# A perceiver block on one core: finer yields for VectorE and ScalarE in the first part, no clearing of the results' table, new estimates in the planner

## The chip, the cores and the metric

The kernel runs on 1 core of a Trainium2 chip. The metric is device time in microseconds (us) of one execution. TensorE is called PE (its weight loads PEld), VectorE DVE, ScalarE ACT, GpSimd POOL, SyncE SP; each has a queue of its own which it works off in order.

## The reference

All is float32. There are 16 sequences of 64 tokens with 256 features, 1024 tokens in all. Six residual steps follow one another:

```python
x = x + xattn0(layernorm(x), ctx)   # 1 head, masked, softmax over 1601 context rows
x = x + mla(layernorm(x))           # 16 heads of 16, causal over 64 tokens, rms-normed q and k
x = x + tile_ffn(layernorm(x))      # one of 8 tiles of weights by position
x = x + xattn1(layernorm(x), ctx)   # 1 head, softmax over 1601 context rows
x = x + ssm(layernorm(x))           # conv of 4, 8 heads, 64 states, selective scan
x = x + moe(layernorm(x))           # 64 experts, 8 of each token, and a shared one
```

The layer norm has no weights: `(x - mean) / sqrt(var + 1e-5)`. The ssm's step size is `dt = softplus(dt_proj + dt_bias)`. The experts compute `silu(x Wg) * (x Wu) Wd`, weighted by the router's normed scores.

## The kernel before, in words

The tokens are worked in 8 groups of 128 (two sequences each). In the first part, to about 600 us, a generator `chain(g)` carries a group through the first four steps: `query(g, "a")` (layer norm, the query transposed into the keys' space), `turn_ctx` for its two sequences' contexts, `cross(g, "a")` (scores, softmax, weighing of the context), `mla(g)`, `clear`, `ffn(g)`, `query(g, "b")`, `cross(g, "b")`. Names of buffers end in `_a` or `_b` for the two cross attentions, in `ml` for mla, `ff` for the tile ffn, `ss` for the ssm, `mo` for the experts. Within cross: `sc` scores, `pa` their exponentials (ACT), `pspa` and `paT` their transposes and the copies of them out of PSUM, `po` the weighed context, `oT` and `py` the output's transpose and product. In mla: `mqk` the normed q and k, `ms` scores, `mee` exponentials, `mpe` and `meT` their transposes, `mo` the result.

Two chains are alive at a time. Beside them run `prepare` (weights of the other steps) and, from group 6's end, `prepare_ssm`, which loads and turns the ssm's input weights (`wl` by SP, `ps_win` on PE), then `inlet(g)` (layer norm, input product, conv pieces `xc`, silu, transposes `ps_xt`) and `sums` (softplus of the step sizes as a polynomial, then `ps_seg` and `ps_sums`), which works on half of the groups at a time. After that come, for each group, the scan (`ps_g`, `gt`, `ps_y`), the routing of its tokens (`route`) and the shared expert; last the experts: the tokens' rows are scattered into a table `xbuf` in device memory (POOL), read back by expert (`xg`), multiplied, and the results scattered into a table `ybuf`, from which each token collects its eight rows.

Which instruction follows which on an engine is settled when the program is built, by a small planner, `drive` (L231). Each generator hands over at its `yield cost, gap`: `cost` is the estimate of the PE time of the piece just emitted, `gap` the estimate of the time until its next piece has its operands. The planner keeps a clock `now`, adds the cost to it, puts the generator aside for `gap`, and goes on with the first that is due:

```python
            c = next((c for c in free if c["at"] <= now), None) or min(free, key=lambda c: c["at"])
            now = max(now, c["at"])
            ...
            cost, gap, sign = (*got, "")[0:3]
            now += cost
            c["at"] = now + gap
```

A third value, "want" or "free", takes or gives back a right that one generator holds at a time. So a yield is at once an estimate and a place where other generators' instructions may come between; between two yields a generator's instructions stand together on every engine.

Lines that the change touches: `zero` and `clear` (L178 to L187: each chain clears, by SP, an eighth of `xbuf` in halves of rows, 544 bytes, and an eighth of `ybuf`, in rows' halves of 512 bytes, from a zero tile); `evac` (L191 to L197, copies out of PSUM turn about on DVE and ACT); `layernorm` (L199: bn_stats, bn_aggr and an add on DVE, a power on POOL for `rs`, then one DVE pass at L213 that waits for it); `inlet` (L267), `sums` (L309; the polynomial L333 to L335, `dt` L338, `ps_seg` L343); `query` (L533), `cross` (L562), its `turn` (L607), `weigh` (L617); `mla` (L742), `ffn` (L931), `chain` (L957), `prepare_ssm` (L986, the loads L997 and L1000, `ps_win` L1041), `route` (L1129).

Of the kernel before, what the change touches and what calls it, by code (L numbers as in the profile page):

```python
# [147 lines left out]
def perceiver_kernel(ctx: ExitStack, tc: tile.TileContext, a: dict, consts: bass.AP, out: bass.AP):  # L148
# [28 lines left out]

    zero = cst.tile([P, DX // 2], F32, name="zero")  # L178
    G.memset(zero, 0.0)
    xbuf0 = xbuf.rearrange("(p n) (c d) -> p (n c) d", p=P, c=2)  # L180
    ybuf0 = ybuf.rearrange("(p n) (c d) -> p (n c) d", p=P, c=2)

    def clear(lo, hi, stage):

        after(nc.sync.dma_start(out=xbuf0[:, 2 * lo : 2 * hi, :], in_=_bc(zero, 1, 2 * (hi - lo))), [stage])
        lo, hi = (n * NTOK * TOPK // NSLOT for n in (lo, hi))
        after(nc.sync.dma_start(out=ybuf0[:, 2 * lo : 2 * hi, :], in_=_bc(zero[:, 0 : D // 2], 1, 2 * (hi - lo))), [stage])  # L187

# [9 lines left out]

    def layernorm(src, name, xn, parted=False):  # L199
        st = small.tile([P, 6], F32, tag="ln_st", name=f"st_{name}")  # L200
        V.bn_stats(st, src)
        mv = small.tile([P, 2], F32, tag="ln_mv", name=f"mv_{name}")
        V.bn_aggr(mv, st)
        ve = small.tile([P, 1], F32, tag="ln_ve", name=f"ve_{name}")
        V.tensor_scalar(ve, mv[:, 1:2], 1e-5, None, ALU.add)  # L205
        rs = small.tile([P, 1], F32, tag="ln_rs", name=f"rs_{name}")
        G.tensor_tensor(rs, ve, neghalf[:, 0:1], ALU.pow)  # L207
# [5 lines left out]
        V.tensor_scalar(to, src, mv[:, 0:1], rs, ALU.subtract, ALU.mult)  # L213
        return xn

# [51 lines left out]
    def inlet(g, tile1, tile2):  # L267
        yield from until(lambda: "winT" in sw)
        xnT, winT = sw["xnT"], sw["winT"]
        tk = slice(g * P, (g + 1) * P)  # L270
        xn = layernorm(x[:, g, :], f"ss{g}", tile1([P, D], f"xn_ss{g}"))
        yield 0, 2.8
        pt = pst([P, 2, P], f"psx_ss{g}")
# [35 lines left out]
    def sums(lo, hi):  # L309

        yield from until(lambda: sw["done"] >= hi)
        dv = sw["dtr"][:, lo:hi, :].rearrange("p g n -> p (g n)")
        n = (hi - lo) * NH


        def sp(name):
            return sw["pool"].tile([P, n], F32, tag=f"sp_{name}", name=f"sp_{name}_{lo}")

        na = sp("na")
        V.scalar_tensor_tensor(na, dv, -1.0, dv, ALU.mult, ALU.min)  # L320
        u = sp("u")
        A.activation(u, na, AF.Exp)
        up2 = sp("up2")
        V.tensor_scalar(up2, u, 2.0, None, ALU.add)
# [12 lines left out]
        dt = sp("dt")  # L337
        V.scalar_tensor_tensor(dt, dv, 0.0, po, ALU.max, ALU.add)  # L338
        yield 0, 4.0
        sg = sw["pool"].tile([n, (NL + 1) * P], F32, tag="sg", name=f"sg_{lo}")  # L340
        for i, w in ((0, 512), (512, 384)):
            pm = psm([n, w], f"ps_seg_{lo}_{i}")
            T.matmul(pm, lhsT=dt, rhs=sw["kmat"][:, i : i + w], start=True, stop=True)  # L343
# [7 lines left out]
    with ExitStack() as p1:  # L351
# [181 lines left out]
        def query(g, lay, beside=None):  # L533
# [3 lines left out]
            xs = x[:, g, :]  # L537
            xn = layernorm(xs, f"xa{nm}", tile1([P, D], f"xn_{nm}"))
            if beside:
                yield from beside  # L540
            else:
                yield 0, 2.7
            xnT = turned(xn, f"xa{nm}")
# [15 lines left out]
            queries[g, lay] = qT, cc, xb  # L559
            yield 1.3, 0.2  # L560

        def cross(g, lay):  # L562
# [31 lines left out]
            for j in range(4):  # L594
# [12 lines left out]
            def turn(j):  # L607
# [47 lines left out]
            V.tensor_tensor(xs, py, xb, ALU.add)  # L655
            yield 0.45, 0

# [84 lines left out]
        def mla(g):  # L742
            wqk, wvo, wkr, vbs = wts["m"]
            xs = x[:, g, :]
            xn = layernorm(xs, f"ml{g}", tile1([P, D], f"xn_ml{g}"))
            yield 0, 2.7
            xnT = turned(xn, f"ml{g}")
# [3 lines left out]
            for c in range(2):  # L751
# [3 lines left out]
                pqs.append(pq)  # L755
            ms = small.tile([P, 32], F32, tag="mms", name=f"mms_{g}")
            V.reduce_sum(ms, sq.rearrange("p c (n d) -> p (c n) d", d=HD), AX.X)
            me = small.tile([P, 32], F32, tag="mme", name=f"mme_{g}")
            V.tensor_scalar(me, ms, 1.0 / HD, EPS_RMS, ALU.mult, ALU.add)

            rr = small.tile([P, 32], F32, tag="mrr", name=f"mrr_{g}")
            V.tensor_scalar(rr.bitcast(I32), me.bitcast(I32), -0.5, 1597463007.0, ALU.mult, ALU.add)
            for i in range(3):
                t = small.tile([P, 32], F32, tag="mt", name=f"mt_{g}_{i}")
                V.tensor_tensor(t, rr, rr, ALU.mult)
                V.scalar_tensor_tensor(t, t, -0.5, me, ALU.mult, ALU.mult)
                V.scalar_tensor_tensor(rr, t, 1.5, rr, ALU.add, ALU.mult)
            qk = tile2([P, 2, 2, P], f"mqk_{g}")
            for c in range(2):
                pv = pqs[c].rearrange("p (j n d) -> p j n d", j=3, d=HD)  # L770
                rv = rr.rearrange("p (c j n) -> p c j n", c=2, j=2)
                for j in range(2):
                    V.tensor_tensor(
                        qk[:, c, j, :].rearrange("p (n d) -> p n d", d=HD), pv[:, 2 * j, :, :], _bc(rv[:, c, j, :], 2, HD), ALU.mult
                    )
            yield 0.7, 0.1
            vs = []
            for c in range(2):
# [12 lines left out]
                vs.append(vb)  # L791
            yield 0.9, 5.0
            ptq = pst([P, 2, P], f"mtq_{g}")
# [22 lines left out]
            for c in range(2):  # L816
                for r in range(4):
                    for b in range(2):
# [5 lines left out]
                            stop=True,  # L824
                        )
            ees, eTs = [], []
            for i in range(2):
# [13 lines left out]
                ees.append(ee)  # L841
            yield 1.2, 3.8, "free"
            for i in range(2):
# [28 lines left out]
            V.tensor_tensor(xs, xs, y, ALU.add)  # L872
            yield 2.0, 0.8

# [56 lines left out]
        def ffn(g):  # L931
            fw, ohb, fb = wts["f"]
            xs = x[:, g, :]
            xn = layernorm(xs, f"ff{g}", tile1([P, D], f"xn_ff{g}"))
            yield 0, 2.7
            xnT = turned(xn, f"ff{g}")
# [192 lines left out]
    def route(g):  # L1129
# [506 lines left out]
```

## Time and profile before

| | us |
|---|---|
| runs | 1113.68, 1122.16, 1114.81; median 1114.81 |
| profiled execution | 1104.11, its span 1102.2 |
| PE busy (82% of the span) | 901.2 |
| PEld busy (62%) | 684.8 |
| DVE busy (54%) | 590.5 |
| POOL busy (25%) | 274.4 |
| ACT busy (25%) | 271.2 |
| mean granted PE clock | 0.879 of full |

An engine's busy time is the sum over its instructions; a wait is the idle time of an engine ahead of an instruction, named by the operation that released it. The profile's slices divide the span by 40, so that one slice is 27.6 us. The share of DMA is the mean busy share of the 16 DMA engines. The transfers that matter here, by their issues on SP: `xbuf<-zero`, 8 of 1632 KB, and `ybuf<-zero`, 8 of 1024 KB.

### The profile page before, as it was taken

What the parts mean: (1) busy time and instruction counts of PE and PEld (TensorE: products, weight loads), DVE (VectorE), ACT (ScalarE), POOL (GpSimd) and SP (SyncE); (2) the same over time, 40 slices, a digit from 0 to 9 for tenths busy, and PEclk for the clock granted to TensorE, in tenths of its full rate; (3) what the DMA queues carried; (4) which work ended last, traced back from release to release, by engine and by line L of the source; (5) the groups of instructions that cost most, each with busy time, mean ns of one, the idle gap of its engine ahead of it and who ended that gap; (6) DMA issues with size and microseconds to landing.
All of it is one profiled execution on the core that took longest, in us unless ns stands there. A gap on an engine that the chain in (4) does not pass through costs nothing. (4 is left out here: it accounts for less than half of the span.)

```text
span 1102.2 us, 16572 instructions
## 1 busy us (share of the span) xinstructions
PE 901.2 (82%) x6242; PEld 684.8 (62%) x6242; DVE 590.5 (54%) x1823; ACT 271.2 (25%) x592; POOL 274.4 (25%) x326
## 2 busy tenths in 40 slices
PE   4887889978799788979867569999999449999955
PEld 3665656645656456556554458888888338888834
DVE  1346454356545554364535874976867773343316
ACT  0213132321332222331313543222210013233310
POOL 0000101001000001001010222266665524655650
PEclk7878998989999899999978878887867669999988
DMA  6411324303613307103430073544411877989336
GB/s 235 172 38 62 100 89 130 120 2 99 184 36 120 97 4 219 59 2 100 103 91 11 28 153 84 118 113 113 113 42 41 277 263 241 304 282 296 116 119 269
DMA packets 99511, 138.99 MB, mean 126 GB/s; under 512 B 10211, under 2 KB 85407, under 8 KB 96358
## 3 DMA queue, kind: packets, MB, share of 16 engines
q1 hardware_dynamic: 84816, 116.36, 34.8%
q0 software_dynamic: 7680, 17.33, 4.6%
q10 hardware_dynamic: 6934, 4.23, 1.5%
q8 instruction: 50, 0.82, 0.3%
q14 instruction: 31, 0.25, 0.1%
HBM read 97.54 MB, written 44.53 MB: 129 GB/s over the span
## 5 line engine op out<-in xcount | busy, mean ns | idle before, releaser
L1481 POOL DMA_INDIRECT ybuf<-yo,goal x96 | 93.5, 974 | 81.3 <-ACT yo L1507 32.7
L1473 PE MATMUL ps_ee<-xT,wq 128*128 128x192 f32 x512 | 96.1, 331 | 0.0
L1115 POOL DMA_INDIRECT xbuf<-xtok,idx x64 | 70.0, 1094 | 71.3 <-DVE idx L1205 48.1
L1473 PEld LDWEIGHTS ps_ee<-xT,wq 128*128 128x128 f32 x512 | 82.5, 191 | 6.5 <-issue 5.0
L620 PE MATMUL po_a<-cn,paT_a 128*64 128x256 f32 (+1 forms) x416 | 59.5, 424 | 22.6 <-ACT mee L840 19.2
L207 POOL TENSOR_TENSOR rs_ff<-ve_ff,neghalf 128x1 f32<-128x1 f32 x8 | 4.4, 548 | 219.1 <-DVE ve_ff L205 211.6
L946 PE MATMUL fpy<-fw,fxm 128*128 128x256 f32 x256 | 58.3, 387 | 0.7 <-DVE fxm L943 0.7
L1337 PEld LDWEIGHTS ps_g<-pc,pb 64*128 64x128 f32 x768 | 51.8, 207 | 10.4 <-issue 5.1
L620 PE MATMUL po_b<-cn,paT_b 128*64 128x256 f32 (+1 forms) x416 | 51.2, 395 | 7.9 <-DVE paT_b L195 4.5
L1337 PE MATMUL ps_g<-pc,pb 64*128 64x64 f32 x768 | 54.7, 295 | 3.0 <-DVE zt L1326 2.0
L620 PEld LDWEIGHTS po_a<-cn,paT_a 128*64 128x64 f32 (+1 forms) x416 | 31.0, 150 | 40.9 <-ACT mee L840 20.1
L946 PEld LDWEIGHTS fpy<-fw,fxm 128*128 128x128 f32 x256 | 49.3, 196 | 8.8 <-PE py_a L654 2.2
L391 PE MATMUL psc<-ct,cn 128*128 128x128 f32 x384 | 52.3, 289 | 2.8 <-DVE cc_a L558 2.8
L391 PEld LDWEIGHTS psc<-ct,cn 128*128 128x128 f32 x384 | 46.9, 150 | 6.6 <-DVE cc_a L558 3.1
L576 PE MATMUL sc_a<-cT,qT_a 128*64 128x512 f32 (+1 forms) x256 | 48.7, 521 | 0.0
L1461 PE MATMUL ps_xT<-ct,xg 128*128 128x128 f32 x192 | 30.9, 289 | 19.7 <-DMA xg<-xbuf 19.7
L1323 POOL TENSOR_TENSOR pc<-cT,e 128x256 f32<-128x256 f32 x48 | 36.1, 787 | 39.3 <-ACT cT L1306 39.3
L1347 DVE COPY_PREDICATED gt<-ct,ps_g 128x256 f32<-128x256 uint32 x96 | 42.3, 545 | 5.2 <-PE ps_g L1337 5.2
L576 PE MATMUL sc_b<-cT,qT_b 128*64 128x512 f32 (+1 forms) x256 | 44.7, 501 | 0.4
L197 ACT COPY cT<-psc 128x512 f32<-128x512 f32 x48 | 28.0, 589 | 66.5 <-PE psc L391 66.5
L620 PEld LDWEIGHTS po_b<-cn,paT_b 128*64 128x64 f32 (+1 forms) x416 | 28.8, 141 | 24.9 <-DVE paT_b L195 5.5
L1475 ACT ACTIVATE hg<-ps_ee 128x192 f32<-128x192 f32 x64 | 21.2, 331 | 93.6 <-PE ps_ee L1473 90.9
(430 smaller groups left out, 1831.9 us busy)
## 6 DMA issues: line engine op xcount, KB each, us to landing
cn<-in_ctx_dram SPq DMA_DIRECT2D x16, 1536.0 KB
e<-segd SPq DMA_DIRECT2D x16, 896.0 KB
xbuf<-zero SPq DMA_DIRECT2D x8, 1632.0 KB
xg<-xbuf SPq DMA_DIRECT2D x16, 816.0 KB
ybuf<-zero SPq DMA_DIRECT2D x8, 1024.0 KB
wq<-in_L_ffn_We_gate_dram SPq DMA_DIRECT2D x16, 512.0 KB
wq<-in_L_ffn_We_up_dram SPq DMA_DIRECT2D x16, 512.0 KB
wq<-in_L_ffn_We_down_dram SPq DMA_DIRECT2D x16, 512.0 KB
```

What stands on the lines that cost most here:

```text
L197: A.copy(dst, src)
L391: T.transpose(ps[:, j, :], cn[:, 4 * q + j, c * P : (c + 1) * P], ident)
L576: T.matmul(sc[b * 64 : (b + 1) * 64, :], lhsT=qT[:, c, b * 64 : (b + 1) * 64], rhs=cTs[2 * g + b][:, c, 512 * j : 512 * j + n], start=c == ...
L620: T.matmul(po[b * 64 : (b + 1) * 64, :], lhsT=paTs[j][:, i, b * 64 : (b + 1) * 64], rhs=cns[2 * g + b][0:r, k, :], start=k == 0, stop=k == KC,
L946: T.matmul(py, lhsT=xm[:, t, c, :], rhs=fw[:, 2 * h + t, c, :], start=h + t + c == 0, stop=h == 3 and t == 1 and c == 1,)
L1115: sct = G.indirect_dma_start(out=xbuf, out_offset=bass.IndirectOffsetOnAxis(ap=idx[:, g, k : k + 1], axis=0), in_=xtok[:, g, 0:DX], in_off ...
L1323: G.tensor_tensor(pc[:, l, :, :].rearrange("p j (k h) -> p j k h", h=1 << l), half(cT, l, 1), half(ev, l, 1), ALU.mult)
L1337: T.matmul(pgs[q][:, i, j, :], lhsT=pb[q * 64 : (q + 1) * 64, l + i, j, :], rhs=pc[q * 64 : (q + 1) * 64, l + i, j, :], start=True, stop=True,
L1347: V.copy_predicated(gt.rearrange("p (j q) (k u h) -> p q j k u h", q=2, u=2, h=h)[:, q, :, :, 1, :], _bc(lvl[:, l + i, :].rearrange("p (k ...
L1461: T.transpose(to, xgs[q][:, 2 * part + s, c * P : (c + 1) * P], ident)
L1473: T.matmul(pe[:, j, :], lhsT=w, rhs=xTs[q][:, i, c, :], start=c == 0, stop=c == 1)
L1481: arr = G.indirect_dma_start(out=ybuf, out_offset=bass.IndirectOffsetOnAxis(ap=goal, axis=0), in_=y, in_offset=None, bounds_check=NTOK * T ...
```

## The change

1. `clear` writes only `xbuf`, in whole rows of 1088 bytes from a zero tile twice as wide; `ybuf` is not cleared any more.
2. `layernorm` is a generator: it yields after its power on POOL and before its last DVE pass. The gap of 2.7 that followed it is split into 1.8 before that pass and 0.9 after it. In `query` of a chain's beginning three pieces of `turn_ctx` come between instead.
3. `sums` yields after the exponential, and twice within the polynomial.
4. `mla` is cut finer: the values (`mxd`, `mv`, `vb`) come ahead of the rms norm; the norm's chain, `mqk`, the scores and each half of the softmax end with yields of their own.
5. In `cross`, the copies `paT` are fixed: odd pieces on ACT, even on DVE.
6. Estimates are new: for a score product 1.95 for 1.75, for half a weighing 0.93 for 1.05, for the output 0.95 for 0.45, for a quarter of the tile ffn 1.75 for 1.0, and others.

```diff
     def clear(lo, hi, stage):
-        after(nc.sync.dma_start(out=xbuf0[:, 2 * lo : 2 * hi, :], in_=_bc(zero, 1, 2 * (hi - lo))), [stage])
-        lo, hi = (n * NTOK * TOPK // NSLOT for n in (lo, hi))
-        after(nc.sync.dma_start(out=ybuf0[:, 2 * lo : 2 * hi, :], in_=_bc(zero[:, 0 : D // 2], 1, 2 * (hi - lo))), [stage])
+        after(nc.sync.dma_start(out=xbuf0[:, lo:hi, :], in_=_bc(zero, 1, hi - lo)), [stage])
...
-    def layernorm(src, name, xn, parted=False):
+    def layernorm(src, name, xn, parted=False, beside=None):
...
         G.tensor_tensor(rs, ve, neghalf[:, 0:1], ALU.pow)
+        if beside is None:
+            yield 0, 1.8
+        else:
+            for _ in range(3):
+                yield next(beside)
...
         V.tensor_scalar(to, src, mv[:, 0:1], rs, ALU.subtract, ALU.mult)
-        return xn
+        if beside is not None:
+            yield from beside
...
         A.activation(u, na, AF.Exp)
+        yield 0, 1.2
...
             V.tensor_scalar(po, po, 2.0 / k, None, ALU.add)
+            if k in (9, 5):
+                yield 0, 1.2
...
         V.scalar_tensor_tensor(dt, dv, 0.0, po, ALU.max, ALU.add)
-        yield 0, 4.0
+        yield 0, 1.5
...
-            yield 1.3, 0.2
+            yield 1.6, 0.4
...
-                    yield 1.75, 0
+                    yield 1.95, 0
...
-            yield 0.3, 2.0, "free"
+            yield 0.35, 2.4, "free"
...
-                evac(paT, pt)
+                (A.copy if j % 2 else V.tensor_copy)(paT, pt)
...
-                        yield 1.05, 0
-                yield 1.05, 0
+                        yield 0.93, 0
+                yield 0.93, 0
...
-            yield 0.45, 0
+            yield 0.95, 0
...
         def mla(g):
...
-            ms = small.tile([P, 32], F32, tag="mms", name=f"mms_{g}")
...
-            yield 0.7, 0.1
+            yield 1.0, 0
             vs = []
...
                 vs.append(vb)
-            yield 0.9, 5.0
+            yield 0.9, 0.3
+            ms = small.tile([P, 32], F32, tag="mms", name=f"mms_{g}")
...
+                V.scalar_tensor_tensor(rr, t, 1.5, rr, ALU.add, ALU.mult)
+            yield 0, 2.8
+            qk = tile2([P, 2, 2, P], f"mqk_{g}")
...
+            yield 0, 1.2
             ptq = pst([P, 2, P], f"mtq_{g}")
...
+            yield 0.7, 0.2
             ees, eTs = [], []
...
                 A.activation(ee, s1, AF.Exp, scale=1.0 / math.sqrt(HD))
                 ees.append(ee)
-            yield 1.2, 3.8, "free"
+                yield (0, 2.0) if i == 0 else (0, 1.0, "free")
...
-                yield 0.55, (1.3, 0.7)[i]
+                yield 0.55, (1.5, 0.7)[i]
...
-            yield 2.0, 0.8
+            yield 1.1, 1.7
...
-                yield 1.0 if h else 1.0, 0
+                yield 1.75, 0
...
-        layernorm(x[:, g, :], f"mo{g}", xr[:, g, :], parted=True)
-        yield 0, 2.8 if g == NG - 1 else 5.0
+        yield from layernorm(x[:, g, :], f"mo{g}", xr[:, g, :], parted=True)
+        yield 0, 1.0 if g == NG - 1 else 3.2
```

The rms norm's lines of mla (from `mms` to `mqk`) are the same before and after; only their place is another.

More of the change, by code (lines that the diff above doesn't have):

```diff
@@ L176, in perceiver_kernel @@
     G.memset(ones, 1.0)
-    zero = cst.tile([P, DX // 2], F32, name="zero")
+    zero = cst.tile([P, DX], F32, name="zero")
     G.memset(zero, 0.0)
-    xbuf0 = xbuf.rearrange("(p n) (c d) -> p (n c) d", p=P, c=2)
-    ybuf0 = ybuf.rearrange("(p n) (c d) -> p (n c) d", p=P, c=2)
+    xbuf0 = xbuf.rearrange("(p n) d -> p n d", p=P)
     def clear(lo, hi, stage):
-        after(nc.sync.dma_start(out=xbuf0[:, 2 * lo : 2 * hi, :], in_=_bc(zero, 1, 2 * (hi - lo))), [stage])
-        lo, hi = (n * NTOK * TOPK // NSLOT for n in (lo, hi))
-        after(nc.sync.dma_start(out=ybuf0[:, 2 * lo : 2 * hi, :], in_=_bc(zero[:, 0 : D // 2], 1, 2 * (hi - lo))), [stage])
+        after(nc.sync.dma_start(out=xbuf0[:, lo:hi, :], in_=_bc(zero, 1, hi - lo)), [stage])
     flip = [0]
@@ L270, in inlet @@
         tk = slice(g * P, (g + 1) * P)
-        xn = layernorm(x[:, g, :], f"ss{g}", tile1([P, D], f"xn_ss{g}"))
-        yield 0, 2.8
+        xn = tile1([P, D], f"xn_ss{g}")
+        yield from layernorm(x[:, g, :], f"ss{g}", xn)
+        yield 0, 0.9
         pt = pst([P, 2, P], f"psx_ss{g}")
@@ L537, in query @@
             xs = x[:, g, :]
[L538 to L542, printed above, removed]
+            xn = tile1([P, D], f"xn_{nm}")
+            yield from layernorm(xs, f"xa{nm}", xn, beside=beside)
+            if not beside:
+                yield 0, 0.9
             xnT = turned(xn, f"xa{nm}")
@@ L744, in mla @@
             xs = x[:, g, :]
-            xn = layernorm(xs, f"ml{g}", tile1([P, D], f"xn_ml{g}"))
-            yield 0, 2.7
+            xn = tile1([P, D], f"xn_ml{g}")
+            yield from layernorm(xs, f"ml{g}", xn)
+            yield 0, 0.9
             xnT = turned(xn, f"ml{g}")
@@ L755, in mla @@
                 pqs.append(pq)
-            ms = small.tile([P, 32], F32, tag="mms", name=f"mms_{g}")
[L757 to L775, printed above, removed]
-            yield 0.7, 0.1
+            yield 1.0, 0
             vs = []
@@ L791, in mla @@
                 vs.append(vb)
-            yield 0.9, 5.0
+            yield 0.9, 0.3
+            ms = small.tile([P, 32], F32, tag="mms", name=f"mms_{g}")
+            V.reduce_sum(ms, sq.rearrange("p c (n d) -> p (c n) d", d=HD), AX.X)
+            me = small.tile([P, 32], F32, tag="mme", name=f"mme_{g}")
+            V.tensor_scalar(me, ms, 1.0 / HD, EPS_RMS, ALU.mult, ALU.add)
+            rr = small.tile([P, 32], F32, tag="mrr", name=f"mrr_{g}")
+            V.tensor_scalar(rr.bitcast(I32), me.bitcast(I32), -0.5, 1597463007.0, ALU.mult, ALU.add)
+            for i in range(3):
+                t = small.tile([P, 32], F32, tag="mt", name=f"mt_{g}_{i}")
+                V.tensor_tensor(t, rr, rr, ALU.mult)
+                V.scalar_tensor_tensor(t, t, -0.5, me, ALU.mult, ALU.mult)
+                V.scalar_tensor_tensor(rr, t, 1.5, rr, ALU.add, ALU.mult)
+            yield 0, 2.8
+            qk = tile2([P, 2, 2, P], f"mqk_{g}")
+            for c in range(2):
+                pv = pqs[c].rearrange("p (j n d) -> p j n d", j=3, d=HD)
+                rv = rr.rearrange("p (c j n) -> p c j n", c=2, j=2)
+                for j in range(2):
+                    V.tensor_tensor(
+                        qk[:, c, j, :].rearrange("p (n d) -> p n d", d=HD), pv[:, 2 * j, :, :], _bc(rv[:, c, j, :], 2, HD), ALU.mult
+                    )
+            yield 0, 1.2
             ptq = pst([P, 2, P], f"mtq_{g}")
@@ L933, in ffn @@
             xs = x[:, g, :]
-            xn = layernorm(xs, f"ff{g}", tile1([P, D], f"xn_ff{g}"))
-            yield 0, 2.7
+            xn = tile1([P, D], f"xn_ff{g}")
+            yield from layernorm(xs, f"ff{g}", xn)
+            yield 0, 0.9
             xnT = turned(xn, f"ff{g}")
```

## The prediction

> **What bounds the kernel now.** First the page's slices: the span of 1102.2 us in 40 slices of 27.6 us, each digit a busy share in tenths, PEclk the clock that TensorE (PE) was granted.
>
> ```profile
> PE   4887889978799788979867569999999449999955
> DVE  1346454356545554364535874976867773343316
> PEclk7878998989999899999978878887867669999988
> DMA  6411324303613307103430073544411877989336
> ```
>
> PE is at 7 to 9 tenths nearly everywhere. It falls at slices 20 to 23 (550 to 660 us), where VectorE (DVE) rises to 8, and at 31 and 32 (860 to 910 us), which the change hardly touches: from the last scan stage on, each engine's order is the same. In the first 650 us PE is the bound, and what can be won there are its waits. Second view: those waits, by the operation that waited and its releaser (total us, times, longest).
>
> ```profile
> PE po_a L620 <- ACT mee L840: 19.2, 4, 4.8
> PE ps_xt L304 <- DVE sp_up L324: 12.1, 2, 7.3
> PE pq_a L550 <- DVE xnT_xaa L195: 8.5, 3, 3.1
> PE ps_win L1041 <- DMA wl<-in_L_attn_W_in_dram: 7.8, 1, 7.8
> ```
>
> All waits of PE to 650 us come to about 118 us, in many small pieces; these four make 47.6. Third view, the timeline (start, duration, operation, idle before), for what stands ahead of the first and third wait. Each engine runs its queue in order.
>
> ```profile
> 236.57 0.69 DVE L838 TENSOR_TENSOR ms<-ms,mmx 128x512 f32<-128x512 f32 x1
> 237.18 0.75 DVE L830 TENSOR_TENSOR ms<-ms,ct 128x256 f32<-128x256 f32 x2
> 237.97 0.69 DVE L837 TENSOR_REDUCE mmx<-ms 128x8 f32<-128x512 f32 x1
> 238.69 0.69 DVE L838 TENSOR_TENSOR ms<-ms,mmx 128x512 f32<-128x512 f32 x1
> 239.30 0.68 DVE L195 COPY paT_a<-pspa_a 128x512 f32<-128x512 f32 x1
> 240.12 3.68 PE L620 MATMUL po_a<-cn,paT_a 128*64 128x256 f32 x16 [4.81 <-ACT mee L840]
> ```
>
> ```profile
> 296.00 0.80 DVE L213 TENSOR_SCALAR xn_ff<-x,mv_ff,rs_ff 128x256 f32<-128x256 f32 x1 [0.73 <-POOL rs_ff L207]
> 296.73 0.41 DVE L195 COPY xnT_xaa<-psx_xaa 128x256 f32<-128x256 f32 x1
> 297.20 1.05 PE L550 MATMUL pq_a<-xnT_xaa,pr_A 128*128 128x128 f32 x7 [3.15 <-DVE xnT_xaa L195]
> ```
>
> po_a needs the two copies of paT_a. They stand behind the softmax of the other chain's mla, both halves of it, so PE idles 4.81 us. And pq_a needs xnT_xaa, whose copy stands behind an xn_ff that itself waits for POOL.
>
> Fourth, SP's queue at 541 to 558 us, where ps_win waits 7.83 us:
>
> ```profile
> 541.77 2.74 SPq L1000 DMA_DIRECT2D wl<-in_L_attn_W_in_dram  x4
> 546.79 0.38 SPq L185 DMA_DIRECT2D xbuf<-zero  x1
> 547.22 4.83 SPq L187 DMA_DIRECT2D ybuf<-zero  x1
> 552.10 5.70 SPq L1000 DMA_DIRECT2D wl<-in_L_attn_W_in_dram  x4
> ```
>
> The last four loads of wl are issued after both clears. In 540 to 560 us the DMA engines are 0.91 busy and PE works 9.35 of 20 us.
>
> **The change, part by part.** The sum is made against the profiled execution, 1104.11 us (span 1102.2), 1.0% below the median of 1114.81; I carry the difference over as it is. I walked each engine's new order, with the durations of before's rows, from one anchor to the next. Negative is faster.
>
> *Two groups of the first part* (a period: 127.75 us from 233.90, 128.15 from 361.65, with 17.8 us of PE waits). Pieces:
> - paT_a: with the mla softmax cut in halves, one half (0.75+0.69+0.69 us of DVE) is no longer ahead of the copies. The wait of 4.81 becomes about 2.75: −2.05.
> - xnT_xaa: its copy no longer stands behind xn_ff and its wait for POOL. The wait (2.70 to 3.15) becomes about 0.9: −2.0.
> - pq_b's wait for xnT_xab, 0.71 to about 0.4: −0.3.
> - ffn after cross a: py_a now comes before psx_ff. Between poT_a and the first fpy stand oT (0.42), py_a (1.13), x+=py_a (0.43), xnT_ff (0.42), bn_stats (0.42) and fxm (0.69), with 0.7 us of handovers, some 4.25 us; before, the distance from poT_a (251.93) to fpy (254.19) was 2.26. +2.0.
> - Scores: psx_xab, pq_b and pc_b now follow one another after sc_a (a wait of 0.6, about xnT's copy and a handover); the second half of qT_b, now on ACT, queues behind four pa_a exps (0.35); the odd paT copies, fixed on ACT, queue behind four pa_b exps (0.78+0.77+0.77+0.41 us; 1.25 of it uncovered); a wait of 1.06 of po_a goes. +1.1.
> - sc_b to po_b: mqk is now behind off_b, and mkb waits behind sm_b for the exps: 3.1 us of waits for 2.7. +0.4. mqk's later place in the cross before: +0.1.
>
> The sum is −0.75 a period; over 3.5 periods **−2.6**. The pieces that give back are as large as those that win, so I allow −9 to +5.
>
> *The clock.* After the 4.81 us wait the next 16 po_a took 3.68 us, and in an undisturbed place 1.95 (16 records): such a wait costs 1.7 us more than itself. The granted clock was 0.51 in 237.70 to 241.10 and 0.50 in the 3.4 us after. The two waits of 2.70 us before pq_a went with a drop each (at 166.1 and 425.5 us); the one of 3.15, cut in two by the clock's windows of 3.41 us, with none. I take two drops saved (3.4 us) against two of the new waits of 1.8 us (ffn, po_b) dropping: **0**, with −4 to +6. The Trainium skill ("TensorE: Matmul & The Clock Gate", HAM oscillation) puts the danger at idle gaps over about 3.4 us. By that rule neither the 2.70 us waits nor the new ones would cost clock at all, and this term would be 0 without balance; the rows with 2.70 us speak against so high a limit.
>
> *Clears.* Per group one issue on SP goes; ybuf's 8 x 1024 KB are no longer written, and xbuf's 8 x 1632 KB go as rows of 1088 bytes for halves of 544. The ybuf clear held SP's queue 4.83 us at 547.22, the xbuf clear 0.38. In the first 540 us nothing on PE waited for a DMA but the first load (pspr_A 5.3), so there this is 0; bounds −3 (context loads sooner) to +1. A packet of 544 bytes took 36 ns at 549 to 552 us, one of 1024 bytes 46 to 51 elsewhere: by these rows a clear's 1632 KB take 4.5 to 5 us of the 16 engines (1536 rows x 46 to 51 ns / 16) where its 3072 halves took 6.9. "DMA: Bandwidth & Descriptors" (Specifications) asks of a descriptor 512 bytes or more for full rate; by that the wider rows alone would bring nothing, and only the bytes left out would count.
>
> *Group 7 beside prepare_ssm.* The four last wl loads are now issued ahead of the last clear, so the wait of 7.83 us goes whole. By the walk from the end of po_b of group 6 (542.15), fpy of group 7 starts after 14.1 us and not 18.8 (560.94), and the last sc_b after about 32 us and not 37.65 (579.80), with new waits inside it (mpe 1.2, psx_ff 2.75, fxm 1.0, qT_b behind the conv pieces 2.2). **−5.6**; bounds −9 to 0.
>
> *Inlets and sums.* From 600 to 660 us PE works 11 to 13 of each 20 us and DVE 14 to 17.6:
>
> ```profile
> 600.00:620.00 20.00, 11.33 (x78) 9.87 (x74) 15.03 (x53) 8.21 (x18) 4.67 (x4) 0.83 0.17 47
> 620.00:640.00 20.00, 12.59 (x70) 9.86 (x70) 14.09 (x47) 7.73 (x17) 3.53 (x3) 0.76 0.31 63
> 640.00:660.00 20.00, 12.98 (x81) 11.20 (x80) 17.59 (x59) 11.38 (x21) 4.51 (x6) 0.82 0.73 154
> ```
>
> (PE, PEld, DVE, ACT, POOL busy, clock, DMA share, GB/s.) Cut finer, the polynomial of sums (L333 to L335) lets the inlets' xc pieces in between, and ps_xt waits less for it (12.1); but DVE's work is not less, so most of it returns as waits for xc. The walk gives 47 to 50 us where 50.3 were: **−1.5**, bounds −3 to +3. Then ps_seg of the second half:
>
> ```profile
> 661.58 3.06 PE L343 MATMUL ps_seg<-kmat,sp_dt 128*32 128x512 f32 x4 [3.77 <-DVE sp_dt L338]
> ```
>
> Now it lies within the first ps_g, whose operands are ready, so 3.77 us of wait go; DVE, idle 5.24 us before gt just after, gets less room to wait in: **−3.5**, bounds −5 to 0.
>
> *Scan and route.* Splitting route's layernorm lets DVE do other work where it stood 19.0 us in 8 waits for rs_mo. PE is busy 36 to 38.6 of 40 us there and waits 2.0 for zt, 1.8 for gt and some 8 before psx_mo: **−1**, bounds −5 to +2. The experts: **0**, same order and transfers.
>
> Sum: −2.6 −5.6 −1.5 −3.5 −1 = −14.2. That is 1089.9 on the profiled execution, and 1114.8 − 14.2 = **1100.6** on the median.
>
> **The rivals.**
> - *Waits only change place.* For: the period's pieces (−4.35 against +3.6), and 600 to 660 us, where DVE has 46.7 us of work in 60. Against: the wl wait is a DMA's and ps_seg's a matter of place. If only half of these two holds (−4.5) and the rest is 0, the time is 1110.
> - *All of it comes.* Period −9, group 7 −9, inlets −3, ps_seg −4, scan −3: −28, 1087.
> - *Slower: the new waits drop the clock.* Three new waits of 1.2 to 1.9 us in a period (ffn, po_b, odd paT). Idle of 1.72 us in a window of 3.41 already went with a drop in the trace (at 104.6). If each drops it, 3 x 3.5 = 10.5 drops of 1.7 to 3.4 us are +18 to +36, less the 14.2: +4 to +22, 1119 to 1137, middle 1127. It turns slower from 8.4 drops of 1.7 us on. Against: an idle of 1.69 us (292.3 to 295.7) had none, and most waits straddle two windows.
> - *The new estimates leave the order as it was.* Nearly every PE row to 650 us has moved, so only the clears would count: 1107 to 1115.
>
> **How the numbers follow.** What a measurement of this kernel can tell from no change is about 1%, 11 us. The forecast's case 0.42, waits that change place 0.26 (with the unmoved order), all of it 0.16, slower by the clock 0.16. The forecast's case by itself spans 1093 to 1107; a third of it lies within 1%. From these: faster by over 1% (below 1103.7) 0.28 + 0.16 + 0.05 = 0.49, slower by over 1% (above 1126) 0.11, within 1% 0.40. The range takes in the middle of "all of it" and the lower part of the slower case: 1085 to 1121.
>
> **What would show it.** In the changed profile: po_a's wait at 2.7 us and no longer for the second mee; no ps_win wait for wl; pq_a waiting under 1 us; psx_ff to fpy with a wait of DVE of some 1.8 us; the period near 127 us; ps_seg of the second half without wait, and DVE above 0.8 in 590 to 650. The prediction is wrong if the period is longer than 128, if the clock of 233 to 490 us falls below 0.96, or if the inlets' stretch from the last sc_b to the first ps_g takes over 84 us (579.8 to 664.6 now).

## The result: slower by 1.3%, and the profile after

| | before | changed |
|---|---|---|
| median of 7 runs, us | 1115.71 (1113.68 to 1122.16) | 1128.41 (1125.75 to 1134.18) |
| ratio | | 1.0127, 95% interval 1.0098 to 1.0157 |
| profiled execution, us (span) | 1104.11 (1102.2) | 1125.75 (1124.0) |
| PE busy, us | 901.2 | 914.1 |
| DVE busy, us | 590.5 | 590.9 |
| mean granted clock | 0.879 | 0.874 |

The forecast was 1101 in a range of 1085 to 1121. The time lies above the range, and the sign is wrong.

The two profiled executions differ by 21.6 us, the medians by 12.7: the chips and executions differ among themselves. Both kernels were therefore profiled once more, on chips 15 and 14 (experiments 1 and 5). The comparisons by stage rest on what both profiles of a kernel agree in.

The page of the changed kernel, its slices (now of 28.1 us):

```profile
PE   4888889978998879977776688889998449989946
PEclk8888999989998999989878767677778669999978
```

Counted from 0, as the prediction counts them, slices 20 to 22 (562 to 646 us) are about as low in PE as before. What is new lies behind them: in slices 23 to 29 (646 to 843 us) the clock stands at 6 or 7 tenths, where it was mostly at 7 or 8 (by the windows view 0.73 for 0.79), and PE is at 8 about as often as at 9.

The waits of PE in the first 650 us of the changed kernel (total us, times, longest):

```profile
PE ps_xt L309 <- DVE xc L305: 10.8, 4, 4.6
PE po_a L627 <- ACT mee L851: 10.0, 4, 2.7
PE psvc_bA L471 <- DVE cols L499: 8.9, 1, 8.9
PE mtq L806 <- DVE mqk L799: 6.9, 5, 1.6
PE pspa_a L619 <- ACT pa_a L604: 6.7, 4, 1.7
PE fpy L958 <- DVE mv_ml L201: 6.6, 4, 1.6
```

Each announced wait is there: po_a's is 2.7 us and no longer 4.8, the long one of pq_a for xnT_xaa is gone, and so is that of ps_win for wl. In their place stand ffn's (1.6, four times) and the one between sc_b and po_b (mtq, 1.6). SP's queue, in which all six remaining pieces of wl now go ahead of the one clear:

```profile
540.49 5.76 SPq L1012 DMA_DIRECT2D wl<-in_L_attn_W_in_dram  x6
547.98 0.38 SPq L184 DMA_DIRECT2D xbuf<-zero  x1
```

Where the time went is told by anchors: the first po_b of groups 0, 6 and 7, the first ps_y (scan 0) and the last ps_pos (end of the routing). Starts and distances in us, each from one profile; "half" is the time that the clock was granted at one half between the first ps_y and the last ps_pos.

| kernel | first po_b | to po_b of 6 | to po_b of 7 | to first ps_y | to last ps_pos | half | rest |
|---|---|---|---|---|---|---|---|
| before | 148.3 | 385.6 | 57.3 | 80.4 | 205.8 | 97 | 224.9 |
| before, second profile | 148.5 | 385.7 | 57.2 | 80.4 | 206.2 | 94 | 224.7 |
| changed | 147.4 | 384.6 | 56.7 | 84.6 | 220.1 | 114 | 230.7 |
| changed, second profile | 152.9 | 384.3 | 56.8 | 84.8 | 220.1 | 118 | 224.1 |

The first part is hardly faster (−1.0 to −1.4 and −0.5). From group 7's weighing to the end of the routing the changed kernel loses 18.4 us: 4.3 ahead of scan 0's ps_y, 14.1 behind it. The 5.8 us of the rest are in the first profile alone. Here is how the scans go. First the timeline of PE in the changed kernel, from scan 0's ps_y on (start, duration, operation, idle before):

```profile
673.21 3.65 PE L1379 MATMUL ps_y<-xtok,gt 128*128 128x64 f32 x16
678.46 1.08 PE L1385 MATMUL ps_yT<-ct,yt 128*128 128x128 f32 x4 [1.59 <-DVE yt L1381]
680.22 3.67 PE L1392 MATMUL ps_o<-woT,yT 128*128 128x256 f32 x8 [0.68 <-ACT yT L1387]
683.72 1.95 PE L1309 MATMUL ps_B<-xnTm,winT 128*128 128x128 f32 x16
```

The same place in the kernel before:

```profile
671.99 1.17 PE L1297 MATMUL ps_B<-xnTm,winT 128*128 128x128 f32 x4
672.95 3.09 PE L1367 MATMUL ps_y<-xtok,gt 128*128 128x64 f32 x14
675.83 2.62 PE L1297 MATMUL ps_B<-xnTm,winT 128*128 128x128 f32 x12
678.29 0.60 PE L1373 MATMUL ps_yT<-ct,yt 128*128 128x128 f32 x4
678.73 1.95 PE L1304 MATMUL ps_C<-xnTm,winT 128*128 128x128 f32 x16
680.51 1.89 PE L1380 MATMUL ps_o<-woT,yT 128*128 128x256 f32 x8
```

Before, the products B and C of scan 1 fill the time in which DVE and ACT turn scan 0's ps_y into yt and yT. In the changed kernel nothing fills it: PE idles 1.59 and 0.68 us, and ps_yT and ps_o run at half the clock (1.08 for 0.60 us, 3.67 for 1.89). B and C come only afterwards. The same holds for scan 1; from scan 2 on the overlap is back. The loss lies in this stretch alone: from the first ps_y of scan 0 to that of scan 3 it is 71.1 us in both profiles of before, and 87.6 and 86.1 in those of the changed kernel; from there to the last ps_pos it is 134.7 and 135.1 before, 132.5 and 134.0 changed. Of these 15.0 to 16.5 us, PE's idle time is 7 to 8 (4.7 us before; 13.1 and 11.6 changed); the other 8 are the same instructions taking longer, at a mean clock of 0.71 and 0.72 for 0.84.

### The profile page after: what moved, and what is told of

Same layout as the page of the kernel before. It is cut to its first block, busy times and chain, and to the rows that moved or that the text cites. A ratio compares the mean times of both kernels' runs of the same rounds, so it can differ in the third digit from the quotient of the medians.

```text
span 1124.0 us, 16573 instructions
## 1 busy us (share of the span) xinstructions
PE 914.1 (81%) x6242; PEld 695.5 (62%) x6242; DVE 590.9 (53%) x1823; ACT 265.8 (24%) x592; POOL 274.6 (24%) x326
## 5 line engine op out<-in xcount | busy, mean ns | idle before, releaser
L1485 PEld LDWEIGHTS ps_ee<-xT,wq 128*128 128x128 f32 x512 | 82.6, 191 | 6.5 <-issue 4.6
L1349 PEld LDWEIGHTS ps_g<-pc,pb 64*128 64x128 f32 x768 | 54.8, 221 | 10.1 <-POOL pc L1335 5.1
L1349 PE MATMUL ps_g<-pc,pb 64*128 64x64 f32 x768 | 57.6, 309 | 2.5 <-DVE zt L1338 1.2
L627 PE MATMUL po_b<-cn,paT_b 128*64 128x256 f32 (+1 forms) x416 | 51.5, 392 | 0.5
L583 PE MATMUL sc_b<-cT,qT_b 128*64 128x512 f32 (+1 forms) x256 | 49.5, 525 | 2.1 <-DVE qT_b L559 1.6
L1335 POOL TENSOR_TENSOR pc<-cT,e 128x256 f32<-128x256 f32 x48 | 36.4, 789 | 42.7 <-ACT cT L1318 40.9
L583 PE MATMUL sc_a<-cT,qT_a 128*64 128x512 f32 (+1 forms) x256 | 46.4, 505 | 0.0
L205 POOL TENSOR_TENSOR rs_ml<-ve_ml,neghalf 128x1 f32<-128x1 f32 x8 | 5.6, 704 | 151.8 <-DVE ve_ml L203 151.8
L1473 PEld LDWEIGHTS ps_xT<-ct,xg 128*128 128x128 f32 x192 | 24.2, 148 | 28.0 <-DMA xg<-xbuf 19.7
```

Of the source, the lines that this page charges most:

```text
L583: T.matmul(sc[b * 64 : (b + 1) * 64, :], lhsT=qT[:, c, b * 64 : (b + 1) * 64], rhs=cTs[2 * g + b][:, c, 512 * j : 512 * j + n], start=c == ...
L627: T.matmul(po[b * 64 : (b + 1) * 64, :], lhsT=paTs[j][:, i, b * 64 : (b + 1) * 64], rhs=cns[2 * g + b][0:r, k, :], start=k == 0, stop=k == KC,
L1335: G.tensor_tensor(pc[:, l, :, :].rearrange("p j (k h) -> p j k h", h=1 << l), half(cT, l, 1), half(ev, l, 1), ALU.mult)
L1349: T.matmul(pgs[q][:, i, j, :], lhsT=pb[q * 64 : (q + 1) * 64, l + i, j, :], rhs=pc[q * 64 : (q + 1) * 64, l + i, j, :], start=True, stop=True,
L1473: T.transpose(to, xgs[q][:, 2 * part + s, c * P : (c + 1) * P], ident)
L1485: T.matmul(pe[:, j, :], lhsT=w, rhs=xTs[q][:, i, c, :], start=c == 0, stop=c == 1)
```

## The experiments

All expectations quoted here were written before the runs. Ratios are to the kernel before on the same chip, with 95% intervals. Three theories: A, the new yields within `sums` move the planner's clock when the scans begin, so that scans 0 to 2 lose their overlap; B, the split of route's layer norm slows the scan; C, the tables (or the experts that read them) cost.

**1. The kernel before, again.** No edit.

> The kernel before, unchanged, for a second profile: the first had a profiled execution of 1104.11 us, 10 us below its own timed runs. If that was luck of the clock in the scan, this profile has a span near 1113 and the stretch from the first ps_y to the last ps_pos (205.8 us in the first profile) is some 5 to 10 us longer; if the scan is stable, it is again within 3 us of 205.8 and the luck lies elsewhere.

Measured: span 1102.8 us, first ps_y to last ps_pos 206.2; ratio 1.0004 (0.9966 to 1.0041). In both profiles the scan of before takes the same time, so the 10 us between the first profile and the timed runs beside it do not lie there. On chip 15 the timed runs are at 1104 us as well (median 1104.66); why the earlier ones are at 1114 is not shown.

**2. The changed kernel with sums as before.**

```diff
         A.activation(u, na, AF.Exp)
-        yield 0, 1.2
...
-            if k in (9, 5):
-                yield 0, 1.2
...
-        yield 0, 1.5
+        yield 0, 4.0
```

> The changed kernel with sums as before (no yields within it, last gap 4.0). Theory A (the yields of sums shifted the planner's clock at the start of the scan, so that the products B of scans 1 and 2 no longer stand within ps_y of the scan ahead): first ps_y to last ps_pos falls from 220 us to 204 to 210, and the time to 0.985 to 1.00 of before. Rival B (the split of route's layer norm slows the scan): that stretch stays at 217 to 222 and the time at 1.01 to 1.015 of before. Rival C (tables and experts): likewise no change in the scan.

Measured: first ps_y to last ps_pos 205.8 us, as A says; but the ratio is 1.0089 (1.0063 to 1.0114), a miss. In the profile the scan is healed, and the time is not. The profile of this kernel has its loss at the start: its first po_b begins at 157.2 us, 9 later than in both profiles of before. DVE's timeline shows one cause:

```profile
45.31 0.17 DVE L890 TENSOR_SCALAR sgp<-sg 8x32 f32<-8x32 f32 x1 [8.64 <-DMA sg<-in_L_ffn_tile_sigs_dram]
45.52 0.18 DVE L892 SCALAR_TENSOR_TENSOR sgn<-sg,sgp 8x32 f32<-8x32 f32 x1
45.63 0.33 DVE L556 TENSOR_SCALAR qT_a<-pq_a,vc_bA 128x128 f32<-128x128 f32 x1
45.89 0.14 DVE L562 TENSOR_TENSOR cc_a<-pc_a,dt_s 128x1 f32<-128x1 f32 x1
```

DVE waits 8.64 us for sg, a load of 8 x 32 numbers for the tile ffn, and the first query's qT_a and cc_a stand behind it. PE then waits 4.30 us for cc_a (2.83 in the first profile of before). That is 1.5 us of the 9; its wait for cols, ahead of that, is 8.62 us for 5.19, and 3.5 us more come between the first sc_a and the first po_b. Why all this kernel's timed runs are slow, and not only the profiled one, is not shown: the profiled run is the fastest of the eight and has the highest mean clock (0.880; the others 0.866 to 0.876), so the others need not have had its scan of 205.8 us; and another kernel had a start of 158 us in the profile without a bad ratio (experiment 7).

**3. The changed kernel, with only the last gap of sums at 4.0.** All new yields stay.

```diff
-        yield 0, 1.5
+        yield 0, 4.0
         sg = sw["pool"].tile([n, (NL + 1) * P], F32, tag="sg", name=f"sg_{lo}")
```

> The changed kernel with all its new yields in sums and only the last gap at 4.0 instead of 1.5; ps_seg of the second half then lies after the second third of ps_g of scan 0, and the scans overlap as before. Theory A: as in the kernel with old sums or 1 to 4 us faster, 0.98 to 1.00 of before; if the yields themselves (longer polynomial) cost, it stays above 1.01. Rival B: 1.01 to 1.015.

Measured: 1.0010 (0.9987 to 1.0034), first ps_y to last ps_pos 209.8 us, po_b of group 7 to first ps_y 77.5. One number takes away the whole loss. The loss ahead of ps_y goes too. PE's timeline there, in the changed kernel:

```profile
656.76 2.00 PE L1349 MATMUL ps_g<-pc,pb 64*128 64x64 f32 x32
661.37 3.16 PE L351 MATMUL ps_seg<-kmat,sp_dt 128*32 128x512 f32 x4 [2.60 <-DVE sp_dt L346]
664.46 7.09 PE L1349 MATMUL ps_g<-pc,pb 64*128 64x64 f32 x64
```

and in this kernel:

```profile
659.15 3.79 PE L1349 MATMUL ps_g<-pc,pb 64*128 64x64 f32 x64
663.84 1.66 PE L351 MATMUL ps_seg<-kmat,sp_dt 128*32 128x512 f32 x4 [0.90 <-DVE sp_dt L346]
665.43 2.00 PE L1349 MATMUL ps_g<-pc,pb 64*128 64x64 f32 x32
```

A third of ps_g is not cover enough for sp_dt: ps_seg still waits 2.60 us, now with ps_g's other two thirds behind it in PE's queue, and these then run at half the clock (7.09 us for 64, where 64 take 3.79). Behind two thirds it waits 0.90.

**4. The kernel before, with the edits of sums alone** (the diff of experiment 2, the other way round).

> The kernel before with the edits of sums alone: its scans lose the overlap as in the changed kernel. Theory A: 1.008 to 1.018 of before, first ps_y to last ps_pos 216 to 224 us. Rival B and C: 0.997 to 1.003.

Measured: 1.0134 (1.0083 to 1.0185), first ps_y to last ps_pos 217.5 us. Around scan 0 the order of PE is that of the changed kernel again, B behind ps_yT and ps_o:

```profile
676.52 3.65 PE L1370 MATMUL ps_y<-xtok,gt 128*128 128x64 f32 x16
681.78 1.09 PE L1376 MATMUL ps_yT<-ct,yt 128*128 128x128 f32 x4 [1.60 <-DVE yt L1372]
683.54 3.78 PE L1383 MATMUL ps_o<-woT,yT 128*128 128x256 f32 x8 [0.68 <-ACT yT L1378]
687.11 2.20 PE L1300 MATMUL ps_B<-xnTm,winT 128*128 128x128 f32 x16
```

The edits of sums alone make the whole loss. Theories B and C are out as its cause.

**5. The changed kernel, again.** No edit.

> The changed kernel, unchanged, beside the others on one chip: 1.010 to 1.016 of before. If the experts' stretch of 161.9 us in its first profile (first ps_xT to last ps_ee; 158.4 before) comes from the table that is no longer cleared, it is 161 to 163 again; if it was the chip or the run, it is 157 to 159.

Measured: 1.0148 (1.0094 to 1.0202); the experts' stretch is 158.2 us. The 161.9 of the first profile was the execution, not the table that is no longer cleared.

**6. The edit of the clears alone, on the kernel before.**

```diff
-        after(nc.sync.dma_start(out=xbuf0[:, 2 * lo : 2 * hi, :], in_=_bc(zero, 1, 2 * (hi - lo))), [stage])
-        lo, hi = (n * NTOK * TOPK // NSLOT for n in (lo, hi))
-        after(nc.sync.dma_start(out=ybuf0[:, 2 * lo : 2 * hi, :], in_=_bc(zero[:, 0 : D // 2], 1, 2 * (hi - lo))), [stage])
+        after(nc.sync.dma_start(out=xbuf0[:, lo:hi, :], in_=_bc(zero, 1, hi - lo)), [stage])
```

> The kernel before with the edit of the clears alone. If the wait of ps_win for wl came from the ybuf clear ahead of it in the queue, it falls from 7.8 us to 2 to 5; from the end of po_b of group 6 to the end of group 7's cross the time falls by at most that. My theory (the gain before po_b of group 7 is lost again ahead of it): po_b6 to po_b7 56 to 57.3 us, time 0.996 to 1.002 of before. Rival (the transfer's end sets that stretch): 52 to 54 us, 0.994 to 0.997.

Measured: po_b of group 6 to po_b of group 7 53.6 us, 3.7 less than before; ratio 0.9981 (0.9955 to 1.0008). The last loads of wl still stand behind the xbuf clear, but the 4.83 us issue of the other is gone, and PE waits 3.87 for them:

```profile
559.11 1.94 PE L1038 MATMUL ps_win<-ct,wl 128*128 128x128 f32 x8 [3.87 <-DMA wl<-in_L_attn_W_in_dram]
```

The stretch came out as the rival had it. The ratio lies where the theory had it, but its interval reaches into the rival's range, so that it does not tell the two apart. By the stretch, without the chains' edits the end of that transfer does set this stretch, and what it wins is kept to po_b.

**7. The edits of the chains alone** (query, cross, mla, ffn; clears, inlet, sums and route as before).

> Only the edits of the chains (query, cross, mla, ffn with their layer norms and estimates); clears, inlet, sums and route as before. Theory: the chains gain about 1 us over po_b0 to po_b6 (385.6 before), the scan is that of before (205 to 207 us), time 0.996 to 1.003 of before. Rival (the chains' edits cost by clock drops): over 387 us and 1.004 or more.

Measured: 1.0000 (0.9967 to 1.0033). First po_b to po_b of group 6 384.3 us for 385.7, po_b of group 6 to that of 7 57.5. The scan took 209.6 us and not 205 to 207, in the same order of PE's instructions as before. Its clock was at one half for 114 us and not 97.

**8. Gap 4.0, and the loads of sg and bs at the start of prepare.**

```diff
         def prepare():
+            sg = stg.tile([NT_FFN, 32], F32, tag="sg", bufs=1, name="sg")
+            nc.scalar.dma_start(out=sg, in_=a["L0_ffn_tile_sigs"])
+            bs = stg.tile([NT_FFN, D], F32, tag="bs", bufs=1, name="bs")
+            nc.scalar.dma_start(out=bs, in_=a["L0_ffn_b"])
+            wts["sgbs"] = sg, bs
             yield from load_L1()
```

> The changed kernel with the last gap of sums at 4.0 and the two small loads of the tile ffn (sg, bs) issued at the start of prepare, about 20 us earlier on ACT's queue; in all profiles so far DVE waited 4.7 to 8.6 us for sg at 35 to 45 us, and PE then 1.8 to 4.3 for cc_a. Theory: both waits go, first sc_a at 40 to 41 us instead of 43, time 0.2 to 0.6% below that of the same kernel without it (0.995 to 0.999 of before). Rival: another of ACT's loads, queued behind, is then waited for, and the time is unchanged.

Measured: 0.9975 (0.9936 to 1.0015). PE no longer waits for cc_a (1.8 us in experiment 3, the same kernel without this edit), but it waits 3.9 us for wT_Wfc, where it waited 2.2, and the first sc_a begins at 42.9 us, not at 40 to 41 (43.0 in experiment 3). In these two profiles another wait takes the gain back before the first scores, and the two ratios cannot be told apart.

**9. The changed kernel, whole, and the scan's gap 11.0 for 12.0.**

```diff
                 A.activation(e[:, j, 0:NL, :], e[:, j, 0:NL, :], AF.Exp, scale=Ac[:, j : j + 1])
-            yield 0, 12.0
+            yield 0, 11.0
```

> The changed kernel with all its edits, and one number more: the gap that the scan names for its load of e is 11.0 instead of 12.0. With it B of scan 1 comes due behind scan 0's ps_y again, in spite of the new yields of sums; ps_seg of the second half then lies behind the last third of ps_g of scan 0. Theory A (the loss is the missing overlap of scans 0 to 2, set by when the planner lets scan 1 begin): first ps_y to last ps_pos 205 to 211 us and 0.995 to 1.003 of before. If the yields of sums cost in themselves, the stretch stays over 215 us and the time at 1.01 or more.

Measured: 1.0028 (0.9996 to 1.0060), first ps_y to last ps_pos 210.2 us. B is back between ps_y and ps_yT:

```profile
679.83 3.65 PE L1379 MATMUL ps_y<-xtok,gt 128*128 128x64 f32 x16
683.27 3.73 PE L1309 MATMUL ps_B<-xnTm,winT 128*128 128x128 f32 x16
686.79 0.84 PE L1385 MATMUL ps_yT<-ct,yt 128*128 128x128 f32 x4
```

Nothing of the change was undone, and 1.2 of the 1.5% (against experiment 5) are gone: the loss lies in the order that the planner chose, not in the yields as such. The stretch ahead of ps_y stays long here (84.3 us).

How one number decides it can be read off the planner's own clock, in its estimates (no measured times). `sums` gives way to scan 0's first third of ps_g, and that third sets the flag for which scan 1 waits. Before, scan 1 gets its turn at 24.2 and asks for its B at 24.2 + 12.0 = 36.2, while scan 0's ps_yT is due at 36.4: B goes first. In the changed kernel `sums` takes its next turn ahead of both scans, scan 0's second third comes before scan 1's turn, and that is 27.2. B is due at 39.2, three later, behind ps_yT and ps_o.

**10. The clears, sums with the last gap at 4.0, and the early loads, on the kernel before** (the diffs of 6 and 8; of the edits of sums the yields alone).

> A version meant to beat both: the kernel before with the clears' edit, the new yields of sums with the last gap at 4.0, and the two small loads sg and bs issued early; chains, inlet and route as before. From the terms measured: clears -3.7 us (po_b6 to po_b7), sums with the overlap kept -3 to 0 (end of that to the last ps_pos), sg -2 to -4: 0.991 to 0.997 of before. If the scan falls into the longer stay at half clock (114 us of it, 209.8 us) the sums bring nothing and it is 0.994 to 0.998.

Measured: **0.9899** (0.9865 to 0.9932), median 1094.97 us beside 1106.84. First po_b 144.2 us, po_b 6 to 7 53.6, to the first ps_y 75.9, to the last ps_pos 207.2. This is faster than both kernels. It is just below the 0.991 to 0.997 that the terms promised, with an interval that reaches into it.

**11. The clears and the early loads alone, on the kernel before.**

> The kernel before with the clears' edit and the early loads of sg and bs alone: clears -3.7 us, sg -2 to -4: 0.993 to 0.997 of before. If sg's wait is only passed on to another load it is 0.996 to 0.999, as with the clears alone.

Measured: 0.9908 (0.9879 to 0.9937); first po_b 146.1 us, po_b 6 to 7 53.6. The clears alone gave 0.9981 (experiment 6, on another chip), so most of the gain goes with the early loads, and it is more than the 2 to 4 us expected of them. Where it arises is not shown: the scan is in its longer form here (209.3 us), and the first po_b comes 2 to 6 us sooner than in before and experiment 6, in a stretch that differs by as much between executions. The sums' yields on top (experiment 10) cannot be told from nothing by the ratio; by the profiles they bring 80.6 to 75.9 us ahead of ps_y.

**12. Gap 4.0, and route's layer norm in one piece.**

```diff
-        yield from layernorm(x[:, g, :], f"mo{g}", xr[:, g, :], parted=True)
-        yield 0, 1.0 if g == NG - 1 else 3.2
+        for _ in layernorm(x[:, g, :], f"mo{g}", xr[:, g, :], parted=True):
+            pass
+        yield 0, 2.8 if g == NG - 1 else 5.0
```

> The changed kernel with the last gap of sums at 4.0, and route's layer norm in one piece as before: tells what its split is worth with the order of the scans held. Rival B (the split costs): first ps_y to last ps_pos 205 to 206 us where it was 209.8, and 0.995 to 0.999 of before. My prediction's term (the split gains 1 us): 210 to 212, and 1.000 to 1.004. No effect: 209 to 210.

Measured: first ps_y to last ps_pos 209.8 us, the same as with the split; 0.9990 (0.9964 to 1.0016). The split of route's layer norm is worth nothing, either way.

The stages of the experiments, as in the table above:

| kernel | first po_b | to po_b of 6 | to po_b of 7 | to first ps_y | to last ps_pos | half |
|---|---|---|---|---|---|---|
| 2 changed, sums as before | 157.2 | 385.1 | 56.3 | 81.5 | 205.8 | 97 |
| 3 changed, gap 4.0 | 150.0 | 385.0 | 56.3 | 77.5 | 209.8 | 114 |
| 4 before, new sums | 151.1 | 385.6 | 57.3 | 82.6 | 217.5 | 118 |
| 6 before, new clears | 151.8 | 385.9 | 53.6 | 80.7 | 205.8 | 97 |
| 7 chains alone | 158.5 | 384.3 | 57.5 | 80.7 | 209.6 | 114 |
| 8 gap 4.0, sg early | 148.7 | 384.5 | 56.7 | 77.7 | 209.9 | 114 |
| 9 changed, scan gap 11 | 153.9 | 384.9 | 56.8 | 84.3 | 210.2 | 115 |
| 10 clears, sums, sg | 144.2 | 384.2 | 53.6 | 75.9 | 207.2 | 104 |
| 11 clears, sg | 146.1 | 385.6 | 53.6 | 80.6 | 209.3 | 114 |
| 12 gap 4.0, old route | 151.9 | 384.7 | 56.7 | 77.8 | 209.8 | 114 |

## Why the prediction was wrong, by its own steps

**The step that failed is "Scan and route: −1, bounds −5 to +2".** It measured +14.1 (205.8 and 206.2 to 220.1, twice). The mechanism that I gave it did not appear: DVE's waits for rs_mo were 19.0 us in all before and 21.6 in the changed kernel, and with the scans' order restored 18.4 with the split (experiment 3) and 18.9 without (experiment 12). I had looked at the scans' busy PE and at these waits, and had compared the orders only from the last scan stage on, where they agree. The order of scans 0 to 2 was at hand and I did not walk it. The edit that moved it is in `sums`, which I had counted only where its own instructions lie. Experiments 3, 4 and 9 show the cause from three sides.

**ps_seg, −3.5.** The premise "operands are ready" held for ps_g and not for ps_seg itself: of 3.77 us of wait 2.60 remained, with two thirds of ps_g behind them at half the clock. From ps_seg to the first ps_y it took 11.8 us for 10.0; with ps_seg behind the second third it takes 4.9 (experiment 3): the mechanism is there, its place was wrong.

**Inlets and sums, −1.5.** The sign is wrong: from the first po_b of group 7 to this ps_seg it is 72.8 and 72.9 us for 70.5. The new yields of sums are not the cause, since experiment 2, with sums as before, has 72.9, and experiment 4, with them alone, 70.7; nor are the chains alone (70.5) or the clears alone (70.7). Which of the other edits, or which two together, make the 2.3 us is not separated. With ps_seg's term I had −5 up to scan 0's ps_y; measured from po_b of group 7 it was +4.3, and −2.9 in experiment 3 (77.5).

**Two groups of the first part, −0.75 a period.** The single waits came as walked: po_a 2.39 to 2.69 us (2.75 foreseen), fpy 1.64 (some 1.8), mtq and ms 1.59 + 1.22 (3.1 in all with a smaller one), and pq_a's long wait gone; only pq_b's for xnT_xab did not shrink (some 0.7 us a time, before and after). The sum has the wrong sign: from the first po_b of group 1 to that of group 6, 2.5 periods, 334.1 us became 336.6 to 336.9, +1.0 a period. PE's idle time there went from 47.8 to 47.0 us, in 44 pieces of more than 0.3 us instead of 36; its busy time went from 286.3 to 289.8, with 27 us at half the clock instead of 24. The waits only changed place, which was a rival, and the busy time grew by more than they fell: the clock accounts for about half of that (3 us more at half of it cost some 1.7, an estimate from ps_o's 3.67 us for 1.89), the rest is not traced. What made the whole part faster by 1.0 to 1.4 is the first step from group 0 to 1 (51.5 to 47.7 us), which I had not walked. One wait I had not foreseen at all: PE stands 2.4 and 1.6 us in the two profiles for cn, a load of the context, most of it at 420 us. The kernel before has no such wait, nor have the clears alone (experiment 6); the chains alone have 2.1 us of it (experiment 7). Two of the prediction's own signs of being wrong came: from group 2 on the period, taken between first po_a, is 128.4 to 130.2 us, where over 128 was the limit, and from the start of the last sc_b to the first ps_g it is 84.1 and 84.3 us, where over 84 was the limit (84.8 before). The third, a clock below 0.96 in these periods, did not (0.96).

**The clock, 0.** For this part near enough (+3 us at one half). The rival that expected 8 to 10 new drops fell: there is one more short drop, at 291.1 us, and the waits just ahead of it are 0.78 and 0.45 us, none of the new ones of 1.6. The drops at 229.7, 359.4 and 489.1 us come where pspa_a's wait of 1.67 us and po_a's of 2.4 to 2.7 follow each other within 6 us, as before (1.67 and 4.8); single waits of 1.6 us elsewhere mostly cost no clock. The Trainium skill ("TensorE: Matmul & The Clock Gate", HAM oscillation) warns of idle gaps over about 3.4 us. No wait of PE in this stretch was as long, and the clock fell five times in it: for this case the limit is too high.

**Clears, 0; group 7, −5.6.** Right for the clears up to 540 us, though PE did wait for one more load there than I said (1.0 us for fwl before, 1.4 after). The wider rows did serve the DMA engines better: a packet of 1088 bytes took 49 ns in the changed kernel (median, 200 to 500 us), one of 544 bytes 34 before, which is 22 and 16 bytes a ns; PE's time did not hang on it there. In group 7 the wait for wl went as foreseen, and fpy of group 7 came 4.9 us sooner after the start of po_b of group 6 (22.2 for 27.1), the last sc_b 5.3 (40.7 for 46.0); from the end of that po_b, as the prediction counts, 15.2 and 33.7 us where it had 14.1 and 32. By po_b of group 7 only 0.5 was left. Half of the gain went in the scores themselves, which ran at a mean clock of 0.68 in the changed kernel and 1.00 before:

```profile
572.63 8.17 PE L583 MATMUL sc_b<-cT,qT_b 128*64 128x512 f32 x32 [1.65 <-DVE qT_b L559]
579.80 5.60 PE L576 MATMUL sc_b<-cT,qT_b 128*64 128x512 f32 x32
```

(The first line is of the changed kernel, the second of before.) From their end to po_b it is 7.8 us for 5.7: two of the inlets' transposes ps_xt and a psx_ss stand there in the changed kernel, and one ps_xt waits 2.49 us for xc. I ended my walk at the start of sc_b and took the rest as given. With the clears alone 3.7 us are kept (experiment 6); with the chains' edits they are not.

**The experts, 0.** Right (158.2 us in the second profile).

No stage that I walked came out below its forecast. A sum of gains, most of them in single waits of under 3 us, was set against an order that is chosen anew as a whole.

## What to carry to other kernels

Where a program is laid out by a planner, any new yield or estimate can shift the planner's clock for all that comes after it, also for work that the edit does not name: compare the whole order of the bound engine, piece by piece, up to the point from which both orders agree to the end. Look first for the places where two pieces of a pipeline overlap, since a shift of three units there cost 14 us here, and a change of one gap by one brought most of it back. An expected gain is only kept if the walk goes on to the next point at which engines wait for each other.

## What the runs showed of the hardware

The clock can stand at one half while PE is nearly always busy. In the kernel before, in two windows that hold nothing but such a stretch (window, length, PE, PEld, DVE, ACT, POOL busy, clock, DMA share, GB/s):

```profile
790.70:804.30 13.60, 12.96 (x68) 12.78 (x66) 9.74 (x41) 2.65 (x5) 7.03 (x7) 0.50 0.55 132
814.60:831.70 17.10, 16.79 (x83) 15.65 (x84) 10.73 (x41) 0.98 (x3) 8.13 (x8) 0.50 0.16 50
```

PE is busy 95 and 98% of them by its instructions, so idle time is not what holds the clock down there. The instructions are the scan's float32 products (ps_B, ps_y, ps_g and others, moving 2 to 256 columns), nearly each with a weight load of its own; which property of them matters is not shown. The same order of PE's operations in the scan took 205.8 us with 97 us at half the clock (before, experiments 2 and 6), or some 209.6 with 114 (experiments 3, 7, 8, 11 and 12). The two part early: after the drop at the first ps_y the next comes 23.9 us later and lasts 3.4 us in the first, and comes 20.5 us later and lasts 10.2 in the second. Which of the two a kernel gets I cannot say; it is 4 us that no reading of the order gives.

Issuing a load can take long: in experiment 2 ACT's queue needed 0.30 us for sg, but 2.27 and 2.10 for the next two small loads, and DVE, which waited for sg, had it only 11.8 us after its issue (33.5 to 45.3). The starts of the kernels, up to the first po_b, spread over 144 to 158 us, more than most edits here are worth.
